# The routing table of the second expert layer: tokens alone, and gates by token

## The chip, the cores and the metric

The kernel runs on one core of one Trainium2 chip. The metric is the time of one execution on the device, in microseconds; lower is better. Runs before the change: 4362.11, 4370.67 and 4372.54 us, median 4370.67.

A core has five engines that run their own instruction streams in order and meet through semaphores: TensorE (PE; PEld is its weight load), VectorE (DVE), ScalarE (ACT), GpSimd (POOL) and SyncE (SP, which here only issues DMA transfers). Transfers issued by SP and ACT go through hardware queues, those issued by POOL (all indirect ones, gathers and scatters by a column of row numbers) through a software queue; all of them share 16 DMA engines.

## The reference, cut to what matters

A macaron block on x of shape 8 x 1024 x 512, that is T = 8192 tokens of 512 values: half an expert layer, attention, half an expert layer again with the same weights.

```python
x = x + 0.5 * _L0_ffn_ref(_layernorm(x), w_router, w_gate, w_up, w_down)
x = x + _L0_attn_ref(_layernorm(x), ...)          # 16 heads of 32
x = x + 0.5 * _L0_ffn_ref(_layernorm(x), w_router, w_gate, w_up, w_down)
```

The expert layer sends each token to the one expert (of 32) with the largest logit. Each expert takes at most C = 320 tokens, in the order of the tokens; those that come later get nothing added.

```python
probs = softmax(xt @ w_router)
top1 = argmax(probs);  gate = probs[top1]
pos = cumsum(onehot(top1))[token, top1] - 1       # place among the expert's tokens
accepted = pos < C
slot = where(accepted, top1 * C + pos, E * C)
buf[slot] = xt
y = (silu(buf @ w_gate) * (buf @ w_up)) @ w_down  # per expert
out = xt + where(accepted, y[slot] * gate, 0)
```

So two things belong to a place (expert, position): the number of the token that has it, and that token's gate. The change is about how these two come to the second layer's experts.

## The kernel before, in words

**First layer.** `front` normalizes and routes all 64 tiles of 128 tokens. It ends with `rows_of`: the token numbers by place, turned by a product on PE (`pt`) into a column of 128 row numbers for each block of 128 places, sorted by how full the experts are. They are kept as `come` (which rows to gather) and `go` (where to scatter). The gates, one per token, go to a DRAM tensor `gates`. Then `experts` branches (`tc.Switch`) on a register that every engine loads from `arm`: it picks one of four lists of widths, for experts that are more or less full. In the branch `Expert.keep` takes over `come` and `go`, and `feed` calls `fetch_gates` for each expert: two or three indirect gathers on POOL, of 128 gates each, by the token numbers in `come` (82 in all).

**Attention.** `Attention.run` goes through stages of 16 slots. In each slot the order of the engines is written out by hand (`manual_schedule`; SP alone is left to the compiler's planner): scores, exponents and weighted sums for one group of four heads, the row maxima of the next, and smaller tasks that are cut up with `yield` and take turns by rank. A task yields `WAIT, n` for n slots, `DVE, n` for a share of DVE's time in a slot, `PE, n` for a place on PE. One such task is `finished(b, half)`, which calls `Block.route` for four tiles of tokens as soon as their logits are there. There are 16 of them; the last two (b = 7, half 0 and 1) come in the last stage and in `ending`.

`route` computes the largest logit, the one-hot matrix, the place of each token (a scan over tiles, two products on PE), from it `slot` (the row of the table), then waits in `scaled` for the rows' mean and variance, and takes the exponent on ACT and from it the gate. Then `put` scatters, with four indirect transfers on POOL, pairs of (token, gate), held in `entries`, to the rows of a DRAM table. The last group (`late`) does it in two steps: the pair with a zero for the gate is scattered once `slot` is known, while the rows are still being finished; the gates go later, in `Late.put`, into a second table `late.table`, from inside the branch.

**Between attention and the second layer.** The last group's `route` also gives the ranks of the experts (`sorted`: `matrix`, `order`, `arm`). `ending` issues the load of the first expert's `w_gate` (1 MB) once `order` is there, and adds the last four tiles' rows to x2. Then comes the branch of `experts`. Inside it `Expert.places` reads the table (96 rows of 128 pairs, L778), copies the half-filled last blocks (L779), turns the token numbers by a product (L788), writes `come` (L790), and yields; the first expert's rows are gathered with `come` (L875), normalized and transposed in `begin`, and its products start (L969). After the gather of the second expert's rows, `late.put` scatters the last gates (L745) and the second table is read (`more`, L783). At the end of the first expert's gated products, `then` calls the last part of `places`: it adds `more`, turns the gates by a second product, and writes `go`. `quarters` does the same again, in small, for the experts whose last block is scattered in quarters.

The start of the kernel fills both tables: `none` and `nothing` are set by POOL and written to DRAM by ACT's queue (L2129, L2132).

## Time and profile before

| | us |
|---|---|
| median of the timed runs | 4370.67 |
| the profiled execution | 4346.86 |
| its span | 4345.1 |
| front of the first layer | 0 to 119 |
| experts of the first layer, to the last scatter | to 877 |
| attention's slots | about 912 to 3549 |
| join: last routing, table, gather, first products | 3549 to 3589 |
| experts of the second layer | to 4345 |

In the profile, times count from the span's start. A line such as `3572.12 0.35 SPq L778 DMA_DIRECT2D slots<-table x1` reads: start, duration (for a DMA, its issue on the queue, not the transfer), engine or queue, line of the kernel, operation, output from input, count; what stands in brackets behind is how long the engine was idle before, and what ended that. In the chain of waits, each piece is released by the one before it. In a table of stretches, each engine has its busy time and, in brackets, its number of instructions; then follow the clock granted to PE as a share, the share of the DMA engines that is busy, and GB/s.

### The profile page before, as it was taken

How to read it: one execution, taken by the hardware profiler on the slowest of the kernel's cores; microseconds unless marked ns; L12 is line 12 of the kernel's file. 1: busy time of each engine (PE TensorE's matmuls, PEld its weight loads, DVE VectorE, ACT ScalarE, POOL GpSimd, SP SyncE). 2: the span in 40 equal slices, each digit the busy share in tenths (PEclk: the TensorE clock that was granted, in tenths of full speed). 3: DMA queues.
4: the chain of work that ended last, by engine and by line, in shares of the span. 5: the costliest groups of instructions: out<-in, count | busy, mean ns of one | idle time of the engine just before them, and what ended most of it. 6: DMA issues, size and time to landing. Idle time of an engine off the chain costs nothing.

```text
span 4345.1 us, 84352 instructions
## 1 busy us (share of the span) xinstructions
PE 4233.0 (97%) x32310; PEld 2407.5 (55%) x32310; DVE 2600.6 (60%) x4964; ACT 2616.9 (60%) x4325; POOL 1401.0 (32%) x1640
## 2 busy tenths in 40 slices
PE   8899999979999999999999999999999979999999
PEld 6566777844444444444444444444444436667777
DVE  8434433356766776876876776776866754344333
ACT  6112221237888888888888888888888842112121
POOL 7344444421222242242232232232232213333332
PEclk9999999989999999999999999999999989999999
DMA  4656666531112212212212212212212116566664
GB/s 157 217 185 204 206 204 229 197 111 48 50 42 71 79 46 65 80 48 65 77 48 65 79 47 65 81 47 63 80 42 60 38 59 206 191 202 202 217 228 162
DMA packets 310835, 495.59 MB, mean 114 GB/s; under 512 B 65049, under 2 KB 99235, under 8 KB 310418
## 3 DMA queue, kind: packets, MB, share of 16 engines
q1 hardware_dynamic: 269698, 412.06, 31.0%
q0 software_dynamic: 39776, 76.77, 5.5%
q8 instruction: 257, 4.21, 0.4%
q14 instruction: 160, 1.31, 0.1%
q10 hardware_dynamic: 944, 1.23, 0.1%
HBM read 379.85 MB, written 87.93 MB: 108 GB/s over the span
## 4 chain that ended last, share of the span: by engine, by line
PE 91%; DVE 3%; issue 2%; ACT 1%; POOL 1%; DMA 1%; POOLq 0%; ACTq 0%; SPq 0%; DVEq 0%
PE s L1240 11%; PE s L1842 11%; PE s L1221 11%; PE gp L969 10%; PE up L969 10%; PE s L1910 10%; PE s L1813 10%; PE yp L1015 9%; PE s L1806 4%; PE tp L957 2%; PE yp L1023 1%; DVE nm L1850 1%; ACT s L1854 1%; PE s L207 1%; DVE st L164 1%
## 5 line engine op out<-in xcount | busy, mean ns | idle before, releaser
L1850 DVE TENSOR_REDUCE nm<-s 128x1 f32<-128x1024 f32 x1024 | 1205.6, 1219 | 541.7 <-PE s L1842 540.3
L1854 ACT ACTIVATE s<-s,nm 128x1024 f32<-128x1024 f32 x1024 | 1114.3, 1088 | 149.9 <-DVE nm L1850 141.3
L974 ACT ACTIVATE sg<-gp 128x320 f32<-128x320 f32 (+7 forms) x256 | 99.5, 389 | 1061.8 <-PE gp L969 1060.8
L1820 ACT ACTIVATE pr<-s 128x512 f32<-128x512 f32 x992 | 538.1, 594 | 230.7 <-PE s L1813 226.8
L1748 POOL TENSOR_TENSOR raw<-raw,a 128x512 f32<-128x512 f32 x125 | 158.6, 1269 | 1312.6 <-DMA rot<-raw 957.3
L1842 PE MATMUL s<-cross,swapped 32*128 32x512 f32 x2048 | 560.4, 607 | 5.4 <-DMA cross<-k 3.1
L1842 PE MATMUL s<-k,q 32*128 32x512 f32 x2048 | 560.1, 603 | 0.0
L1822 ACT ACTIVATE pr<-s 128x1024 f32<-128x1024 f32 x528 | 542.9, 1031 | 19.7 <-PE s L1813 19.7
L1813 PE MATMUL s<-q,k 32*128 32x512 f32 x4096 | 538.4, 590 | 0.0
L1221 PE MATMUL s<-hT,wqk 128*32 128x128 f32 (+3 forms) x4720 | 503.3, 324 | 8.8 <-ACT pr L1820 4.9
L1910 PE MATMUL s<-pr,big 128*32 128x512 f32 x4096 | 492.7, 598 | 0.5 <-ACT pr L1822 0.5
L969 PE MATMUL gp<-bT,wg 128*128 128x272 f32 (+7 forms) x1984 | 488.7, 389 | 0.0
L969 PE MATMUL up<-bT,wu 128*128 128x272 f32 (+7 forms) x1984 | 484.9, 387 | 0.0
L1221 PEld LDWEIGHTS s<-hT,wqk 128*32 128x32 f32 (+1 forms) x4720 | 299.1, 129 | 286.1 <-ACT pr L1820 101.6
L1015 PE MATMUL yp<-wd,a 128*128 128x512 f32 x992 | 445.9, 592 | 0.0
L969 PEld LDWEIGHTS gp<-bT,wg 128*128 128x128 f32 x1984 | 371.6, 190 | 87.4 <-issue 21.4
L969 PEld LDWEIGHTS up<-bT,wu 128*128 128x128 f32 x1984 | 374.4, 190 | 70.3
L996 DVE TENSOR_TENSOR a<-sg,up 128x320 f32<-128x320 f32 (+7 forms) x256 | 110.6, 432 | 491.0 <-PE up L969 431.5
L1842 PEld LDWEIGHTS s<-k,q 32*128 32x128 f32 x2048 | 243.2, 183 | 102.0 <-DVE raw L1689 36.3
L1910 PEld LDWEIGHTS s<-pr,big 128*32 128x32 f32 x4096 | 106.7, 109 | 347.6 <-ACT pr L1820 187.4
L1019 DVE SCALAR_TENSOR_TENSOR ys<-yp,gates,x 128x512 f32<-128x512 f32 x128 | 96.1, 751 | 336.9 <-PE yp L1015 336.9
L1842 PEld LDWEIGHTS s<-cross,swapped 32*128 32x128 f32 x2048 | 224.4, 183 | 119.3 <-DVE raw L1689 22.8
(307 smaller groups left out, 5394.8 us busy)
## 6 DMA issues: line engine op xcount, KB each, us to landing
wg<-in_w_gate SPq DMA_DIRECT2D x62, 1024.0 KB
wu<-in_w_up SPq DMA_DIRECT2D x62, 1024.0 KB
wd<-in_w_down SPq DMA_DIRECT2D x62, 1024.0 KB
rot<-raw SPq DMA_DIRECT2D x1000, 32.0 KB
all<-in_x SPq DMA_DIRECT2D x32, 512.0 KB
xt<-first_rows SPq DMA_DIRECT2D x64, 256.0 KB
swapped<-q SPq DMA_DIRECT2D x256, 64.0 KB
xr<-first_rows SPq DMA_DIRECT2D x64, 256.0 KB
```

The costliest lines, as they stand in the source:

```text
L969: nc.tensor.matmul(acc, w[:, k, f * P : (f + 1) * P], to.bT[:, k, 0:width], start=(k == 0), stop=(k == s.KD - 1),)
L1015: nc.tensor.matmul(yp, a[:, f, i * P : (i + 1) * P], wd[:, f, :], start=(f == 0), stop=(f == KF - 1),)
L1221: self.nc.tensor.matmul(acc[a : a + w, lo:hi], one[:, a : a + w], two[:, lo:hi], start=(i == 0), stop=(i == len(terms) - 1),)
L1240: self.nc.tensor.matmul(bank[a : a + w, 0 : to - at], one[:, a : a + w], two[:, at:to], start=(i == 0), stop=(i == len(terms) - 1),)
L1806: nc.tensor.matmul(sb[:, h, :], self.ones16[at : at + 3, :], row[at : at + 3, :], start=True, stop=False,)
L1813: nc.tensor.matmul(sb[:, h, :], k[at, t * P : (t + 1) * P], q[at, n * 512 : (n + 1) * 512], start=False, stop=True,)
L1820: nc.scalar.activation(pr[:, h, :], sb[:, h, :], AF.Exp)
L1822: nc.scalar.activation(pr, sb, AF.Exp)
L1842: nc.tensor.matmul(sa[:, m, :], (own if here else swapped)[at, at_q], ka[at, m * 512 : (m + 1) * 512] if here else cross[at, :], start=Tru ...
L1850: nc.vector.tensor_reduce(nm[:, j, h : h + 1], flat, AX.X, ALU.max, negate=True)
L1854: nc.scalar.activation(flat, flat, AF.Exp, bias=nm[:, j, h : h + 1], accum_out=se[pair][:, j, odd : odd + 1],)
L1910: nc.tensor.matmul(po[at : at + HD, :], self.v[b][t + j][:, c * P + at : c * P + at + HD], prs[h // 2 * 2][:, h % 2, :], start=(j == 0), s ...
```

## The change

The second layer is given its places and gates in the form that the first layer has.

- The table holds the token alone (one number in place of two); it is filled with `none` alone, and the second table, `Late`, `entries` and `places` are gone.
- `route` has new arguments. For all groups but the last, `put` comes right after `scaled` and ahead of exponent and gate; for the last, it comes once `slot` is known, as before. The gates of every group are kept in `gate` and stored to a DRAM tensor by token, `gates[1]`: by SP, one slot after the gate's instructions, and by ACT for the last group. Each store writes 128 x 4 single numbers.
- A new function, `Attention.placed`, is called after `finish` and ahead of the branch: it reads the table, copies the half blocks, turns the tokens by one product and writes `come` and `go` into tiles that last through the branch.
- In the branch, `Expert.keep` serves both layers; `fetch_gates` now also runs for each of the second layer's experts (82 more gathers of 128 gates on POOL), and nothing is turned any more after the first expert's gated products. `quarters` turns one matrix, not two.

The diff, cut to its core:

```diff
@@ Block.constants
-        self.entries = pool.tile([P, self.NT, 2], F32, name="entries")
+        self.gate = pool.tile([P, self.NT], F32, name="gate")
...
-        nc.vector.tensor_copy(self.entries[:, :, 0], self.token)
@@ Block.route
-        row = self.entries[:, t0 : t0 + G, :]
+        gate = self.gate[:, t0 : t0 + G]
...
                 nc.gpsimd.indirect_dma_start(
                     out=table[t0 + j],
                     out_offset=bass.IndirectOffsetOnAxis(ap=slot[:, j : j + 1], axis=0),
-                    in_=row[:, j, :],
+                    in_=self.token[:, t0 + j : t0 + j + 1],
                     in_offset=None,
                 )
...
-        if late:
-            nc.vector.memset(row[:, :, 1], 0.0)
-            yield from put()
+        r = None if last else (yield from scaled())
+        yield from put()
         if ordered:
             at_once(ordered())
-        r = yield from scaled()
+        if last:
+            r = yield from scaled()
         yield DVE, 0.3
         nc.vector.tensor_tensor(ex, ex, over_e(r), ALU.mult)
         nc.scalar.activation(ex, ex, AF.Exp)
         yield WAIT, 1
         yield DVE, 0.7
-        gate()
-        if not late:
-            yield from put()
+        nc.vector.tensor_reduce(se, ex, AX.X, ALU.add)
+        nc.vector.reciprocal(se, se)
+        nc.vector.tensor_scalar(gate, se, 0.5, None, ALU.mult)
+        if not last:
+            yield WAIT, 1
+        (nc.scalar if last else nc.sync).dma_start(store, gate)
@@ Block.experts
-                if kept:
-                    expert.keep(kept)
-                else:
-                    places = expert.places(table, late)
-                    next(places)
+                expert.keep(kept)
                 now = expert.gather(0, widths[0])
...
-                if late:
-                    late.put(nc)
-                    next(places)
-                    then = lambda: next(places, None)
@@ Expert.feed
-        if self.of is not None:
-            self.fetch_gates(now)
+        self.fetch_gates(now)
...
-        if then:
-            then()
@@ Attention.run
                 self.ending()
                 self.finish()
+                self.placed()
                 self.apart()
...
+    def placed(self):
+        nc, s, pool, E, n = self.nc, self.s, self.ranking, self.s.E, self.s.last
+        R = s.NB * E
+        rows = pool.tile([R, P], F32, name="rows")
+        come, go = (pool.tile([P, R], I32, name=name) for name in ("come", "go"))
+        self.kept = SimpleNamespace(rows=rows, come=come, go=go, gates=self.gates)
+        nc.sync.dma_start(
+            rows, self.whole_table[0 : s.NS, :].rearrange("(r s) c -> r (s c)", s=P)
+        )
+        nc.vector.tensor_copy(rows[R - E : R, n:P], rows[R - E : R, 0:n])
+        pt = self.take()[:, 0:R]
+        nc.tensor.matmul(pt, rows, self.ranks[0], start=True, stop=True)
+        nc.vector.tensor_scalar(come, pt, float(s.T - 1), None, ALU.min)
+        nc.vector.tensor_copy(go[:, 0 : R - E], pt[:, 0 : R - E])
+        for i in range(2):
+            p = slice(i * n, (i + 1) * n)
+            nc.vector.tensor_scalar(
+                go[p, R - E : R], pt[p, R - E : R], 2.0, float(i), ALU.mult, ALU.add
+            )
@@ Attention.finished
-            late=self.late if last and half else None, spaced=not last,
+            self.gates[first * P : (first + 4) * P, :].rearrange("(t p) c -> p (t c)", p=P),
+            spaced=not last, last=last and half,
@@ tile_macaron
-    table = dram.tile([s.NS + T, 2], F32, name="table")
-    gates = dram.tile([T, 1], F32, name="gates")
+    table = dram.tile([s.NS + T, 1], F32, name="table")
+    gates = [dram.tile([T, 1], F32, name=f"gates{i}") for i in range(2)]
...
-        nothing = pool.tile([P, s.NS // P], F32, tag="nothing", bufs=1, name="nothing")
-        nc.gpsimd.memset(nothing, 0.0)
-        nc.scalar.dma_start(
-            late.table[0 : s.NS, :].rearrange("(p r) c -> p (r c)", p=P), nothing
-        )
```

## The prediction

> **What bounds the kernel now.** I read the page first (part 4, the chain that ended last), then the busy time by stage, then the timeline and the waits around the two joins. The profiled execution took 4346.86 us (span 4345.1 us and 1.76 us around it); the median of the timed runs is 4370.67 us, 23.8 us above. The sum is made against the profiled time, and that offset is added unchanged.
>
> The chain by engine, from the page: TensorE carries nearly all of it.
>
> ```profile
> PE 91%; DVE 3%; issue 2%; ACT 1%; POOL 1%; DMA 1%; POOLq 0%; ACTq 0%; SPq 0%; DVEq 0%
> ```
>
> By stretch (columns: length, busy PE, PEld, DVE, ACT, POOL with counts, clock, DMA share, GB/s): first layer, attention, the join behind it, second layer.
>
> ```profile
> 131.00:895.00 764.00, 749.71 (x3359) 533.60 (x3358) 290.55 (x775) 157.59 (x280) 330.43 (x351) 0.99 0.62 205
> 950.00:3549.00 2599.00, 2578.44 (x24716) 1238.65 (x24718) 1870.49 (x2966) 2210.96 (x3562) 707.35 (x839) 1.00 0.22 59
> 3549.00:3589.00 40.00, 13.71 (x49) 7.80 (x42) 22.20 (x90) 3.80 (x7) 16.04 (x19) 0.63 0.49 155
> 3589.00:4346.00 757.00, 745.78 (x3346) 530.72 (x3345) 282.93 (x752) 152.67 (x273) 250.10 (x260) 0.99 0.61 200
> ```
>
> In attention PE is busy 99.2%, so nothing that leaves PE fed changes it. In the 40 us of the join PE works 13.7 us: only there, at the very start and in the first expert can this change pay.
>
> The join in the timeline: first and last scatter of the last four tiles, the weight load, the table's read, its copy, the places, the first gather, the first product.
>
> ```profile
> 3561.27 0.96 POOL L307 DMA_INDIRECT table<-entries,late_slot  x1 [0.30 <-DVE both L639]
> 3561.64 0.42 SPq L671 DMA_DIRECT2D big<-in_w_gate  x1
> 3565.06 0.95 POOL L307 DMA_INDIRECT table<-entries,late_slot  x1 [0.30 <-issue]
> 3572.12 0.35 SPq L778 DMA_DIRECT2D slots<-table  x1
> 3574.45 0.22 DVE L779 COPY slots<-slots 32x128 f32<-32x128 f32 x1 [3.90 <-DMA slots<-table]
> 3575.96 0.26 DVE L790 TENSOR_SCALAR come<-pt 128x96 int32<-128x96 f32 x1 [1.29 <-PE pt L788]
> 3577.11 1.03 POOL L875 DMA_INDIRECT x<-x,come  x1 [8.23 <-DMA all<-x]
> 3588.51 3.33 PE L969 MATMUL gp<-bT,big 128*128 128x320 f32 x8
> ```
>
> The queue SP itself stood for the landing of these scatters (total, times, longest):
>
> ```profile
> SPq L778 <- DMA table<-entries,late_slot: 5.6, 2, 5.1
> ```
>
> So the path is: slots of the last tiles (written 3558.10 to 3558.26) -> POOL free (3561.27) -> scatters landed (some 3570.8) -> read -> turn -> gather -> product. The branch is not on it: SP was at the read by 3565.7 (3570.8 less the 5.1 us wait).
>
> **The change, part by part.**
>
> *The start.* The chain runs through ACT's issue of the second table's zeros:
>
> ```profile
> 6.41 1.14 ACTq L2132
> 7.58 1.28 ACT L546
> ```
>
> ACT then works without a gap to 27.5, and DVE waits for it twice (2.25 us at 19.36, about 1.4 at 27.72) before it becomes the engine that paces the front. The issue goes, and with it the fill `nothing` (0.17 us on POOL) and a 0.20 us copy on DVE; ACT can load its table at about 6.2. Bounds: 0 (the first products, at 8.25, are late next) to -1.4. I take -1.0, since DVE's two waits can absorb more than that.
>
> *The 15 groups routed before the last.* Their scatters (4 x 1.0 us on POOL each) go ahead of exponent and gate; POOL's waits for the gate, 84.4 us over 15 groups, disappear. POOL has 707 us of work in 2599, so this is worth 0. Added are 15 stores on SP, each 512 single elements of 4 B. SP's issue: a weight load of as many runs takes 0.37 to 0.42 us. On the DMA engines: the window 3556 to 3561.6 has nothing but 8 B scatters,
>
> ```profile
> q0 software_dynamic: 109, 0.00, 1.6%
> ```
>
> 1.6% of 16 x 5.6 us over 109 packets is 13 ns each, so 512 packets are 0.42 us of each engine. Behind a store on SP stand the copies for the rotation, `swapped` and `cross`, whose reader is PE. In 2637 us of attention PE waited for `cross` once, 3.1 us; so they arrive with time to spare, and 0.8 us per store is hidden: 0. If that cover fails: 15 x 0.8 = 12 us. A store may also stand on SP for its gate; POOL stood 5.6 us per group for it: that is the slower rival below.
>
> The Trainium skill (DMA: Bandwidth & Descriptors, Rules for kernel authors) speaks against such a store: a strided last dimension becomes one descriptor per element, and it advises making it contiguous. The same page (Anatomy of one DMA) puts 2.0 us of fixed cost on a DMA; 15 of them in sequence on the path would be an estimated 30 us and a slower kernel. The row above, and that nobody waits for a store until 3592, make it nothing.
>
> *Scatters of the last two groups.* Those of the group before the last no longer wait for the gate (3555.65): POOL is free after the power at 3550.64, their slots are there since 3549.2. So they run from 3550.9 to 3555.9 instead of 3556.11 to 3560.96, and the last four start at about 3558.4 and 3562.2, not 3561.27 and 3565.06: 2.8 us earlier. Their landing is what counts. Scatters issued up to 3560.01 landed in 2.1 us; the four from 3561.27 on took 5.6 to 7.6, median 6.6, beside 2 MB of `w_gate` and rows of x2 (282 to 400 GB/s from 3564 to 3570). The last one now starts 0.6 us behind the load's issue, nearest to the row at 3562.54, so I give it 6.6 us: landed 3568.9, read issued 3569.4 with half a us of semaphores. Bounds: landed in 2.1 us, the read at 3565; or in 7.6 with today's 1.3 us of semaphores, at 3571. Gain 2.7, between 1 and 7.
>
> *Read and turn ahead of the branch.* The read (48 KB, was 96) meets the end of that traffic: 2.33 us today in a quiet moment, up to 4.8 (a gather under load); I take 2.6, a loss of 0.3. Copy, product and `come` keep their 1.8 us. POOL passed its branch by 3571.4 and needs `come` at about 3573.8, so its first gather follows 0.9 us later as today. What is moved past: SP's branch now follows the read and took 3.6 us (3562.06 to 3565.7), so the two loads `all` (0.5 MB each) go out at about 3573.4 beside the gathers rather than ahead of them. The first layer has this order, and there gather to product took 11.9 us (119.11 to 130.99) against 11.4 here: a loss of 0.5 to 1.0, I take 0.7. DVE's branch follows its writing of `go`; it is at most 3.9 us (3570.54 to 3574.45), against some 4.3 us until the first gathered rows land, so it is just covered; at worst +1.5. PE's has 8 us. ACT gets the last store (at 3570.6, 0.5 us) ahead of its branch and is needed at 3580. Join: -2.7 + 0.3 + 0.7 = -1.7, bounds -5 and +1.5.
>
> *The experts.* The first layer fetches its gates by token already, so it is the measurement of the new form. There the first expert runs from the last half of its products straight into the transposes and the down product:
>
> ```profile
> 147.15 2.15 PE up L969 x8
> 149.30 0.66 PE tp L957 x6
> 149.96 3.43 PE yp L1015 x8
> ```
>
> The second layer has the turn of the gates in between:
>
> ```profile
> 3604.76 2.17 PE up L969 x8
> ...
> 3607.51 0.21 DVE slots L785
> ...
> 3607.99 0.48 PE pt L788 x2
> ```
>
> From the first `gp` to the last scatter the first layer takes 746.27 us (131.04 to 877.31), the second 748.37 (3588.57 to 4336.94). The 2.10 us are this turn and the second product of the quarters, and both go. The 82 gate fetches (0.98 us and 0.27 of issue on POOL, 103 us) lie beside PE: POOL's 330 of 764 us in the first layer shows that they fit. If POOL were full, they would cost up to 103. -2.1, between -2.4 and -1.5. On POOL the four late scatters (3591.24 to 3596.1) also leave the way of the next expert's weight load; it was in time before: 0.
>
> Sum: -1.0 + 0 - 1.7 - 2.1 = -4.8 us: 4342.1 for the profiled execution, 4365.9 for the median.
>
> **The rivals.**
> 1. *The join gives nothing.* The scatters land when the weight load lets them, whenever issued, and the branches of DVE and SP become visible behind the turn. For it: a 5.1 us wait for landing, beside 1 MB of weights; against it: 2.1 us for those issued a us before the load. -1.0 - 2.1 + 0 to 1.5: 4367.6 to 4369.1.
> 2. *Everything early lands early.* Last scatter in 2.1 us, the join takes -5, the start -1.4, and the earlier POOL saves a few of PE's 20 us of waits in attention: 4358 to 4362.
> 3. *Slower: SP is held up in attention.* A store is queued ahead of the rotation's copies and stands for its gate. The price is the 5.6 us that POOL stood per group, 84 us in all; it decides once more than 18 of them reach PE (1.2 per group), since -4.8 must be undone and 13 passed. A third of it gives 4394. Against it: PE's one wait of 3.1 us for `cross`; for it: nothing in this trace bounds how SP's order comes out.
> 4. *The fetches fill POOL* in the second layer: up to +103; the first layer speaks plainly against it.
>
> **How the numbers follow.** Chances: the forecast 0.53, rival 1 0.23, rival 2 0.11, rivals 3 and 4 0.13. What a measurement here tells from no change is about 0.3%, 13 us. The forecast and rival 1 lie within it but for the spread of runs (4362.1 to 4372.5); of rival 2 most of it too. Faster 0.11, same 0.75, slower 0.14. The forecast's own range, -5 to +1.5 at the join with the other bounds and 4 us of spread, is 4357 to 4373. The range reaches up toward rival 3 to leave out no more than 2 in 10, and below through rival 2: 4354 to 4382.
>
> **What would show it.** Right: ACT's first table load near 6.2; scatters of the last group from 3558, the read near 3569, the first gather near 3575 and the first `gp` near 3586 (each less about 1 for the start); the first `up` of the second layer followed by `tp` at once; 746 us from first `gp` to last scatter. Wrong: the read still at 3572 (landing set by the weights), DVE's first statistics late after landed rows (branch exposed), PE waits on `cross` or `swapped` in attention with SP standing for `gate`, POOL without gaps in the second layer.

## The result, and the profile after

The changed kernel took 4414.73 us (median of 4 runs, 4410.22 to 4415.05), the kernel before beside it 4368.27 us (4 runs): ratio 1.0104, 95% interval 1.009 to 1.0118. It is 46 us slower. The forecast was 4365.9 us in a range of 4354 to 4382, with a chance of 0.14 for slower.

One thing is needed to read the numbers below. The runs were made on six occasions, each with its own runs of the kernel before, and these fall into two kinds: the kernel before took 4367 to 4368 us on four of them (the result's among them) and 4354 us on two (single runs there reach down to 4345). I call them H and L. All ratios are between runs of one occasion; the few differences in us that cross from the result's occasion to the next are between two with the same 4368 us for the kernel before. The profile that the prediction used, 4346.86 us, is like an L profile; the timed runs beside it were like H. A later profile of the kernel before in kind H (4370.82 us) is the one to put beside the profile after (4415.05 us, span 4413.3).

The chain of the profile after reads nearly as before; TensorE still carries it.

```profile
PE 90%; DVE 4%; issue 3%; ACT 2%; DMA 1%; POOL 1%; SPq 0%; POOLq 0%; DVEq 0%; ACTq 0%
```

By stretch (length, busy PE, PEld, DVE, ACT, POOL with counts, clock, DMA share, GB/s), the changed kernel: first layer, attention, join, second layer.

```profile
131.00:895.00 764.00, 750.19 (x3360) 534.02 (x3359) 291.33 (x776) 157.92 (x280) 330.74 (x351) 0.99 0.62 205
950.00:3608.00 2658.00, 2619.32 (x24700) 1253.92 (x24699) 1878.00 (x2959) 2211.68 (x3564) 707.07 (x839) 0.99 0.22 58
3608.00:3661.00 53.00, 18.12 (x75) 8.78 (x74) 26.21 (x103) 5.80 (x10) 16.45 (x19) 0.60 0.46 112
3661.00:4413.00 752.00, 745.36 (x3342) 530.64 (x3340) 283.58 (x744) 152.74 (x272) 326.68 (x338) 1.00 0.61 202
```

The same for the kernel before in kind H, without the first layer:

```profile
950.00:3568.00 2618.00, 2595.56 (x24701) 1245.44 (x24703) 1873.51 (x2958) 2211.02 (x3564) 708.09 (x839) 0.99 0.21 59
3568.00:3612.00 44.00, 18.00 (x73) 9.43 (x69) 24.67 (x100) 5.27 (x8) 15.60 (x19) 0.64 0.46 144
3612.00:4368.00 756.00, 746.75 (x3347) 531.42 (x3346) 283.57 (x753) 153.25 (x274) 250.86 (x260) 0.99 0.60 200
```

PE has as many products in attention (24700 and 24701) and takes some 40 us more for them. To cut the stages alike in each kernel I take as marks the start of the last scatter into `first_rows`, the start of PE's last product that reads `mrow`, the first product of the second layer and the start of its last scatter, and call what follows to the end of the span the tail:

| profile | us | to the first mark | attention | join | second layer | tail |
|---|---|---|---|---|---|---|
| before, as predicted from | 4346.86 | 877.3 | 2668.0 | 43.2 | 748.4 | 8.2 |
| before, kind H | 4370.82 | 877.6 | 2690.3 | 44.1 | 748.9 | 8.1 |
| after, kind H | 4415.05 | 878.2 | 2730.4 | 51.8 | 747.0 | 5.9 |
| difference, both H | 44.2 | +0.6 | +40.1 | +7.7 | -1.9 | -2.2 |

So the loss is in attention, where the sum had 0, and in the join, where it had -1.7. What was forecast for the experts came. One caution for the column on attention: in every profile its first stretch (from the mark to the last `rot<-s,a` on DVE) takes either 40.1 to 40.5 or 43.3 to 43.8 us, long before the first of the scatters and stores in question. That alone is worth 3 to 4 us between two profiles. The two in kind H here both have the long form, the one that the prediction used has the short one.

Inside attention the loss shows in one group of products of PE (engine, operation, tiles, shape, count; busy us and mean ns; idle time before them and what ended it), between 1000 and 3500 us. After:

```profile
L1758 PE MATMUL s<-mrow,ones 3*128 3x512 bf16 x1936 | 211.0, 385 | 25.1 <-ACT s L1806 14.4 <-issue 10.7
```

Before, kind H:

```profile
L1806 PE MATMUL s<-mrow,ones 3*128 3x512 bf16 x1976 | 211.4, 385 | 11.9 <-ACT s L1854 11.6 <-issue 0.2
```

New are 10.7 us in which PE stood for "issue", nothing that the profile shows. They lie in six of the eight batches (the kernel takes its tokens in eight batches of 1024), each time inside a row of six scatters that POOL runs one behind the other (1887.23 to 1893.59 in the second batch, 1.26 us apart). Before, POOL waited for each group's gate between them; now it comes from the wait for the rotation's rows, finds six scatters ready and runs them at once. The planned spacing of one slot between two scatters orders the instructions, it does not space them in time.

The join after, in the timeline: the store of the last group but one, the weight load, the last scatter, the last store, the read of the table, its copy, the first gather, the first product.

```profile
3619.42 0.37 SPq L343 DMA_DIRECT2D gates<-gate  x1
...
3624.79 0.41 SPq L668 DMA_DIRECT2D big<-in_w_gate  x1
...
3625.65 0.95 POOL L301 DMA_INDIRECT table<-token,slot  x1 [0.30 <-issue]
...
3634.08 0.38 ACTq L343 DMA_DIRECT2D gates<-gate  x1
3637.64 0.33 SPq L1290 DMA_DIRECT2D rows<-table  x1
...
3646.81 0.19 DVE L1293 COPY rows<-rows 32x64 f32<-32x64 f32 x1 [12.76 <-DMA rows<-table]
...
3649.07 1.03 POOL L807 DMA_INDIRECT x<-x,come  x1 [16.69 <-DMA all<-x]
...
3660.44 1.97 PE L901 MATMUL gp<-bT,big 128*128 128x320 f32 x3
```

```profile
3625.00:3628.00 3.00, 2.50 (x3) 0.41 (x2) 2.86 (x7) 0.00 (x0) 1.30 (x2) 0.50 0.62 38
3628.00:3631.00 3.00, 0.00 (x0) 0.00 (x0) 2.86 (x7) 0.00 (x0) 0.00 (x0) 0.50 0.38 18
3631.00:3634.00 3.00, 0.00 (x0) 0.00 (x0) 1.36 (x9) 0.31 (x1) 1.04 (x1) 0.50 0.78 81
3634.00:3637.00 3.00, 0.00 (x0) 0.00 (x0) 0.05 (x1) 0.00 (x0) 0.00 (x0) 0.50 1.06 402
```

The second fence is the stretches from 3625 to 3637, columns as above. The scatters went out at 3621.88 to 3625.65, 13.2 us behind the end of attention instead of 16.0 in the profile that the prediction used: 2.8 us earlier, as forecast (3.6 us against the profile in kind H). But behind the store the weight load moves 38, 18 and 81 GB/s instead of the 282 to 400 that it had before, and reaches 402 only at 3634. SP stood for the landing of the scatters 12.2 us in all (5.6 before):

```profile
SPq L1290 <- DMA table<-token,slot: 12.2, 3, 6.8
```

The read then goes out 3.6 us behind the store of the last group on ACT's queue and takes from 3637.64 to 3646.81, 9.2 us, where it took 2.33 before. Two stores are at work here; the run with one of them alone, further down, shows what belongs to the first.

### The profile page after: what moved, and what is told of

Read it like the earlier page. It is cut to its first block, busy times and chain, and to the rows that moved or that the text cites. A ratio compares the mean times of both kernels' runs of the same rounds, so it can differ in the third digit from the quotient of the medians.

```text
span 4413.3 us, 84426 instructions
## 1 busy us (share of the span) xinstructions
PE 4278.9 (97%) x32306; PEld 2424.4 (55%) x32306; DVE 2610.0 (59%) x4956; ACT 2617.6 (59%) x4325; POOL 1477.4 (33%) x1716
## 4 chain that ended last, share of the span: by engine, by line
PE 90%; DVE 4%; issue 3%; ACT 2%; DMA 1%; POOL 1%; SPq 0%; POOLq 0%; DVEq 0%; ACTq 0%
PE s L1170 11%; PE s L1794 11%; PE gp L901 10%; PE s L1151 10%; PE up L901 10%; PE s L1862 10%; PE s L1765 10%; PE yp L944 9%; PE s L1758 4%; PE tp L889 2%; PE yp L952 1%; DVE nm L1802 1%; ACT s L1806 1%; DMA table<-token,slot 1%; PE s L206 1%
## 5 line engine op out<-in xcount | busy, mean ns | idle before, releaser
L1794 PE MATMUL s<-cross,swapped 32*128 32x512 f32 x2048 | 576.9, 614 | 4.9 <-issue 3.1
L1794 PE MATMUL s<-k,q 32*128 32x512 f32 x2048 | 572.5, 610 | 1.1 <-DVE raw L1641 1.1
L1765 PE MATMUL s<-q,k 32*128 32x512 f32 x4096 | 555.5, 596 | 2.9 <-issue 2.7
L1151 PE MATMUL s<-hT,wqk 128*32 128x128 f32 (+3 forms) x4720 | 513.3, 327 | 4.6 <-DVE hT L1571 3.8
```

Of the source, the lines that this page charges most:

```text
L1151: self.nc.tensor.matmul(acc[a : a + w, lo:hi], one[:, a : a + w], two[:, lo:hi], start=(i == 0), stop=(i == len(terms) - 1),)
L1765: nc.tensor.matmul(sb[:, h, :], k[at, t * P : (t + 1) * P], q[at, n * 512 : (n + 1) * 512], start=False, stop=True,)
L1794: nc.tensor.matmul(sa[:, m, :], (own if here else swapped)[at, at_q], ka[at, m * 512 : (m + 1) * 512] if here else cross[at, :], start=Tru ...
```

## The experiments

Two suspects were in the trace after, the rows of scatters and the single-element stores, and each can be taken away alone. The first theories, as they are on record: A, rows of back-to-back scatters hold up PE; B, 512 single-element stores block the DMA engines.

### Taking each away (occasion of kind H, before 4368.19 us)

**The scatters behind the gate again.** The scatter's source `pos` is written behind the gate, so that POOL waits for it as before; the stores stay.

```diff
-                    in_=self.token[:, t0 + j : t0 + j + 1],
+                    in_=self.token[:, t0 + j : t0 + j + 1] if last else pos[:, j : j + 1],
...
-        yield from put()
+        if last:
+            yield from put()
...
+            nc.vector.scalar_tensor_tensor(
+                pos, gate, 0.0, self.token[:, t0 : t0 + G], ALU.mult, ALU.add
+            )
+            yield from put()
```

> The changed kernel, with the scatters of all groups but the last made to wait for the gate again, as in the kernel before (they take the token from a tile that is written after the gate); the stores of single gates stay. Theory A (bursts: six scatters back to back on POOL hold up PE's next refill of instructions, PE starves and its clock drops): no refill later than about 15 us, attention from 2663 back to about 2600 us, the join still 8 us longer than before; about 4355 us where the changed kernel takes 4414. Theory B (stores: 512 single elements written to 2 KB of DRAM block the DMA engines, the refill among them): attention stays near 2660, about 4414.

Measured: 4376.33 us, ratio 1.0018 (1.0008 to 1.0027). Attention 2696.4 us instead of 2730.4, join still 52.2. The profiled execution (4382.19) is the slowest of ten. The waits for the gate that the prediction valued at 0 were worth some 38 us against the result's 4414.73.

**The gates turned on PE and stored once.** The 16 stores go; one transpose in `placed` and one store of 64 rows of 512 B take their place. The scatters stay early.

```diff
-        if not last:
-            yield WAIT, 1
-        (nc.scalar if last else nc.sync).dma_start(store, gate)
...
+        gt = self.take()[0 : s.NT, 0:P]
+        nc.tensor.transpose(gt, s.gate, s.ident)
+        turned = pool.tile([s.NT, P], F32, name="turned")
+        nc.scalar.copy(turned, gt)
+        nc.scalar.dma_start(self.gates.rearrange("(t p) c -> t (p c)", p=P), turned)
```

> The changed kernel, with the sixteen stores of single gates taken out; the gates of all groups are turned once on PE after the table's places and stored in 64 runs of 512 B. Scatters run early as in the changed kernel. Theory A: attention still about 2660 us with clock dips, only the join gains: weight load and table read no longer stand, read to landing 2 to 3 us and not 9, so some 8 to 10 us less than the changed kernel, about 4405. Theory B: the dips go too, about 4345 to 4355.

Measured: 4389.81 us, ratio 1.005 (1.0033 to 1.0066). The join is 38.9 us, 5.2 less than before in kind H: without the stores the earlier scatters do bring what the prediction hoped for. Attention is 2714.2 us, still 24 more than before in kind H (27 behind its first stretch, which is short here).

**Both edits.**

> The changed kernel with both edits: scatters after the gate, and gates turned and stored in runs of 512 B. Both theories: attention about 2600 us and a join no longer than before; by the terms of the prediction that held (first expert and quarters -2, join -2 to 0) 2 to 4 us under the kernel before. If attention stays long here, neither theory is right.

Measured: 4357.88 us, ratio 0.9979 (0.9968 to 0.9989): faster than both kernels. Attention 2683.8, join 42.1. Against this kernel the early scatters cost 31.9 us (4389.81 less 4357.88) and the stores 18.5 us (4376.33 less 4357.88). The changed kernel, which has both, is 46 + 10 = 56 us above it, so the two together cost about 6 us more than their sum (this last number goes across two occasions).

**The kernel before with its scatters early.** The gate is left out of the scattered pairs but for the last 512 tokens, so that the scatter need not wait for it. No stores.

```diff
-            nc.vector.tensor_scalar(late.gate if late else row[:, :, 1], se, 0.5, None, ALU.mult)
+            nc.vector.tensor_scalar(late.gate if late else se, se, 0.5, None, ALU.mult)
...
-        if late:
-            nc.vector.memset(row[:, :, 1], 0.0)
-            yield from put()
+        r = None if late else (yield from scaled())
+        yield from put()
```

> The kernel before with one part of the change alone: the scatters of pairs (8 B) of all groups go ahead of exponent and gate. No stores of single gates. It leaves out the gates of all tokens but the last 512 (their place in the table is zero). Theory A: six scatters back to back, attention 50 to 65 us longer than before, about 4420. Theory B, and also a theory that only 4 B entries do it: attention as before, about 4365.

Measured: 4398.91 us, ratio 1.0064 (1.0046 to 1.0081), attention 2722.3 us. The early scatters alone, put into the old kernel, make most of the loss: 30.7 us here with 8 B each, 31.9 with 4 B in the comparison above, so size and table make no difference that can be seen.

### What in the row? (occasion of kind L, before 4353.68 us)

**The last batch's first half early as well**, the candidate for the best version. In the other batches the scatters stay behind the gate.

```diff
-        if last:
+        if not spaced:
             yield from put()
...
-        if not last:
+        if spaced:
             nc.vector.scalar_tensor_tensor(
```

> The kernel with both edits (4357.88), and in the last batch alone the first half's four scatters go ahead of the gate again, as in the change. In it nothing follows that PE could starve on for long: the bursts of the other seven batches stay spaced by their gates. Theory A (back-to-back scatters cost only where PE needs refills under load; the join gains from earlier scatters): attention as with both edits, 2684 +-5; the join 39 us (38.9 with the gates turned) instead of 42.1; time 4354 to 4356. Rival (a burst costs some 4 us wherever it stands, also in the last batch): 4358 to 4360.

Measured: 4344.12 us, ratio 0.9982 (0.9973 to 0.9991); join 39.9 us, as expected. The time itself is not what was expected, because the occasion was another.

**No planned spacing behind the gate** (both edits kept): rows of four, late.

```diff
-                if j and spaced:
-                    yield WAIT, 1
```

> The kernel with both edits (4357.88), but the four scatters of a half are issued one after the other behind the gate, with no slot of the planner between them. They are as late as before, but bursts of four, 14 of them. Theory A (it is the row of scatters without a gap that delays PE's refill, whenever it comes): 7 bursts of six cost some 30 us with the gates turned, 4.3 each; by the number of scatters 14 bursts of four cost up to 2.9 each: 4375 to 4400, with refill gaps of 16 us and more beside the bursts and PE stalled by issue. Rival (going ahead of the gate is what costs, a different order on DVE, ACT or SP): as with both edits, 4355 to 4363.

Measured: 4346.29 us, ratio 0.9987 (0.9978 to 0.9996). Rows of four, no pause of PE in any.

**POOL held without DMA** (both edits kept): four powers of 128x4 where the change has its early scatters.

```diff
+        else:
+            held = narrow("held")
+            for j in range(G):
+                if j and spaced:
+                    yield WAIT, 1
+                nc.gpsimd.tensor_tensor(held, s, self.power[:, 0:G], ALU.pow)
```

> The kernel with both edits (4357.88), and where the change put its early scatters, four powers of 128x4 on POOL instead (1.04 us each by the row of rstd, the length of a scatter, but no DMA); the scatters stay behind their gates. POOL gets 60 more instructions and 62 us. Theory A1 (the scatters' DMA elements stand ahead of PE's refill): as with both edits, 4355 to 4365, no refill gap over those seen there. Theory A2 (POOL is held for some 7 us without a gap, and something that PE needs waits for POOL): attention +30 as with the gates turned, 4383 to 4393.

Measured: 4345.67 us, ratio 0.9988 (0.9979 to 0.9997), attention 2671.7. No loss. (Only four powers stood in a row, 4 us, since a scatter with its gate came between them and the rest.)

**The kernel before once more.**

> The kernel before once more, unchanged, for its profile: the profile that the prediction used was 4346.86 us, below every timed run (4360 to 4372). If the stalls of PE at the refill that the change shows come by chance in the kernel before as well, an execution of about 4365 us has two to four of them in attention, with attention of 2680 to 2690 us in place of 2668, and the other stages the same within 1 us. If the offset lies elsewhere (the start or the layers), attention stays at 2668.

Measured: 4355.13 us, attention 2675.2; no pause in it. The three results look as if theory A and its rival A2 were settled. The next occasion showed that they were not.

### The control (occasion of kind L, before 4353.61 us)

**The early scatters diluted**, a power on POOL behind each (on top of the kernel with the gates turned):

```diff
                     in_offset=None,
                 )
+                if spaced:
+                    nc.gpsimd.tensor_tensor(held, s, self.power[:, 0:G], ALU.pow)
```

> The kernel with the gates turned (scatters early, no single stores: 1.005 of before, attention 2714), and behind each early scatter a power of 128x4 on POOL (1.04 us, no DMA). The row of six then has a scatter every 2.3 us instead of every 1.26; POOL is held longer, 14 us instead of 7.5, and has 15.8 us until the rotation needs it next. Theory A (it is how closely the scatters' DMAs follow each other that stalls PE): the pauses of some 0.4 to 1.1 us between PE's instructions inside the row go, the time is that of the kernel with both edits, 0.997 to 0.999 of before. Rival E (what costs is that the scatters come ahead of the gate, with another order on POOL, DVE and ACT): 1.004 to 1.006 of before, as with the gates turned.

Measured: 4344.89 us, ratio 0.9983 (0.9973 to 0.9993).

**A row of eight, late, as planned** (both edits kept): in POOL's order the first half's scatters are put behind the second half's gate.

```diff
+            if not spaced:
+                put()
+            elif t0 % 8 == 0:
+                self.first_half = put
+            else:
+                self.first_half()
+                put()
```

> The kernel with both edits, but the first half's four scatters of a batch wait for the second half's gate, and all eight go out in a row: late, and closer together than in any kernel so far. Theory A: the pauses of PE come back in every batch but the last, 7 rows of eight against 6 rows of six: 1.004 to 1.010 of before. Rival E (early is what costs): 0.997 to 0.999 of before. The kernel with rows of four late lost nothing (0.9987), so a third way is that the length of the row does not matter in this place, which also gives 0.997 to 0.999; only together with the kernel diluted above are the two told apart.

Measured: 4345.00 us, ratio 0.9987 (0.9977 to 0.9996). But the edit did not make rows of eight. The order on POOL changed; the first half's scatters still wait for their own gate alone, and the second half's for theirs. In seven batches the trace has two rows of four, 8 to 13 us apart, as in the second batch, where the fourth and the fifth scatter are:

```profile
1879.49 0.96 POOL L299 DMA_INDIRECT table<-pos,slot  x1 [0.31 <-issue]
1884.26 0.96 POOL L299 DMA_INDIRECT table<-pos,slot  x1 [3.81 <-DVE pos L341]
```

So this run is a second one on rows of four, and no row longer than six was tried in attention.

**The gates turned, the same kernel as above.**

> The kernel with the gates turned once more, unchanged, beside the others on the same chip: 1.005 of before, with PE's pauses inside six rows of scatters (18 us of PE's gaps in attention against 6 in the kernel before). If the stalls belong to a chip and not to the kernel, 0.997 to 0.999.

Measured: 4346.28 us, ratio 0.9986 (0.9976 to 0.9995), where the same kernel had 1.0050. Its six rows of six are there (14.2 to 20.6 us behind the first scatter of the second batch, 14.6 to 21.0 the first time), and PE does not pause in them. So on an occasion of kind L no row shows a cost, and the runs on rows of four, on POOL held and on dilution, all made there, tell nothing about what in the row matters. The control belonged on the same occasion from the start.

The pair is the best view of the cost, though: one kernel, the same place of the program. Set side by side by the order of DVE's instructions, the two executions keep step up to the first row of six (-0.03 us), part by 6.1 to 8.8 us at each of the six rows, and then keep step again (43.6 and 43.8 us): the whole difference in attention lies at the rows. Kind H, the second batch (start, us, engine, line, operation):

```profile
1881.78 0.96 POOL L301 DMA_INDIRECT table<-token,slot  x1 [0.30 <-issue]
1881.82 1.06 PE L1148 MATMUL s<-hT,wqk 128*32 128x128 f32 x32
...
1883.04 0.96 POOL L301 DMA_INDIRECT table<-token,slot  x1 [0.30 <-issue]
...
1883.48 0.37 PE L1760 MATMUL s<-mrow,ones 3*128 3x512 bf16 x1 [0.60 <-issue]
...
1884.20 0.37 PE L1760 MATMUL s<-mrow,ones 3*128 3x512 bf16 x1 [0.36 <-issue]
1884.30 0.95 POOL L301 DMA_INDIRECT table<-token,slot  x1 [0.30 <-issue]
...
1885.63 0.37 PE L1760 MATMUL s<-mrow,ones 3*128 3x512 bf16 x1 [1.05 <-issue]
...
1886.35 0.58 PE L1760 MATMUL s<-mrow,ones 3*128 3x512 bf16 x1 [0.35 <-issue]
...
1886.36 2.66 PE L1767 MATMUL s<-q,k 32*128 32x512 f32 x5
...
1888.05 0.35 DVE L1643 TENSOR_SCALAR raw<-s,bias 128x128 f32<-128x128 f32 x1 [5.18 <-remote]
```

and the stretches around it:

```profile
1882.00:1884.00 2.00, 1.25 (x34) 0.79 (x26) 0.87 (x2) 1.62 (x4) 1.70 (x2) 1.00 0.39 69
1884.00:1886.00 2.00, 0.74 (x2) 0.09 (x1) 0.00 (x0) 0.00 (x0) 1.39 (x2) 1.00 0.51 63
1886.00:1888.00 2.00, 1.65 (x7) 1.02 (x9) 0.00 (x0) 0.00 (x0) 0.52 (x1) 0.60 0.01 0
...
1890.00:1892.00 2.00, 2.00 (x8) 0.50 (x2) 0.36 (x1) 1.17 (x2) 0.00 (x0) 0.50 0.03 8
```

Kind L:

```profile
1874.82 0.95 POOL L301 DMA_INDIRECT table<-token,slot  x1 [0.30 <-issue]
1874.93 1.06 PE L1148 MATMUL s<-hT,wqk 128*32 128x128 f32 x32
...
1875.92 0.40 PE L1760 MATMUL s<-mrow,ones 3*128 3x512 bf16 x4
...
1876.08 0.96 POOL L301 DMA_INDIRECT table<-token,slot  x1 [0.30 <-issue]
1876.15 1.03 PE L1767 MATMUL s<-q,k 32*128 32x512 f32 x8
1876.16 0.34 DVE L1643 TENSOR_SCALAR raw<-s,bias 128x128 f32<-128x128 f32 x1
```

```profile
1876.00:1878.00 2.00, 2.00 (x21) 0.82 (x21) 1.04 (x5) 1.68 (x4) 1.62 (x2) 1.00 0.80 115
```

In kind L the four products of `mrow` run within 0.40 us, and at 1876.16 DVE reads what PE left. In kind H they start at 1883.48, 1884.20, 1885.63 and 1886.35; with their weight loads (1882.81, 1883.50, 1884.91, 1886.33) that is about one instruction per 0.7 us, with no wait on record. DVE, which needs only the 32 products from 1881.82, goes on at 1888.05, 5 us late. PE's signal for these products is on record at 1887.96, 5.1 us behind their (modelled) end; in kind L it comes 0.05 us behind. So it was not the issue alone that was held up, but also work that PE, by its records, had already begun. The stretches show what follows: PE busy 1.25, 0.74 and 1.65 of 2 us, and then the clock at 0.50, with a PE that is busy throughout and works at half speed. Setting the two kernels' products side by side by their place in the program, the lag that this row adds is 3.8 us at the last of the four `mrow` products and 7.6 us once the clock is back: half of the cost is the pauses, half the clock. That answers the period of a batch, 330.8 us in kind H and 323.3 in kind L, 7.5 us.

The clock's record has it at 0.50 from 1886.4 to 1893.2, 6.8 us (the stretches above have 0.60 from 1886 to 1888, 0.50 after that), behind 3.5 us of broken work (1882.88 to 1886.35) in which PE ran three products of 0.37 us. The Trainium skill (TensorE: Matmul & The Clock Gate, the section on the HAM clock gate) has PE at half its clock after an idle window of some 3.4 us. The length agrees; but here PE was not idle, only little used.

The pair also corrects theory A where it named PE's refill of instructions (packets of 16 KB on the queue that the profile calls instruction, one per 12.9 us). In kind H the refills around this row start at 1872.40 and 1890.03. PE issues without the pauses again from 1886.35, with no refill in between. So a refill did not end the pauses; that the next one is late fits PE's slow progress.

**One store at the join put back** into the candidate, on SP, into a tensor that nobody reads.

```diff
         nc.vector.tensor_scalar(gate, se, 0.5, None, ALU.mult)
+        if not spaced and not last:
+            yield WAIT, 1
+            nc.sync.dma_start(store, gate)
```

> The kernel with both edits and the last batch's first half early (0.9982 of before, join 39.9 us), with one of the change's 16 single-element stores put back: that of the last batch's first half, on SP ahead of the expert's weight load, into a tensor that nobody reads. The prediction had such a store at 0.42 us of the engines. Theory B (512 single elements of 4 B slow the loads and scatters behind them for some ten us): the weight load creeps for 8 us or more, the scatters land late, the join takes 47 to 52 us, the time rises by 7 to 12 us: 1.000 to 1.001 of before. Rival (the store was harmless; the last store, on ACT, or the scatters themselves made the join long): join 40 to 41 us, 0.998 of before.

Measured: 4346.55 us, ratio 0.9988 (0.9979 to 0.9998); join 43.5 us against 39.9 without the store. SP's total wait for the scatters, with the store and without:

```profile
SPq L1296 <- DMA table<-token,slot: 11.2, 3, 5.3
```

```profile
SPq L1293 <- DMA table<-token,slot: 7.4, 3, 4.7
```

3.6 us for one store, also in kind L: neither the 7 to 12 of theory B nor nothing. The slow load is there with this one store, at 35 GB/s in the second stretch behind its issue; without the store it has 268:

```profile
3565.00:3568.00 3.00, 0.00 (x0) 0.00 (x0) 2.83 (x7) 0.00 (x0) 0.00 (x0) 0.50 0.92 35
```

```profile
3570.00:3573.00 3.00, 0.00 (x0) 0.00 (x0) 2.86 (x7) 0.00 (x0) 0.00 (x0) 0.96 0.78 268
```

The join alone shows the cost (one profile each; without single stores and with the last scatters early it is 38.6 to 39.9 in the five profiles with the new table). The two times, 2.4 us apart and from two occasions, do not.

### The change again (two occasions of kind H, before 4367.45 and 4367.00 us)

> The changed kernel once more, unchanged. Theory D (the pauses of PE inside the rows of scatters come on some chips and not on others; the single-element stores cost something on each): on a chip like that of the last two calls the attention is 5 to 20 us longer than before (the stores alone), the join 47 to 52 us, the layer 1.5 us shorter, in all 1.001 to 1.005 of before, and no pause of 0.7 us and more per instruction on PE inside a row; on a chip like the first 1.009 to 1.011, as measured. Rival (the stores and the early scatters together make the pauses, and the kernel with the gates turned was only near the edge): 1.008 to 1.011 on either chip, with pauses.

Measured: 4404.60 us, ratio 1.0076 (1.0057 to 1.0095), a little under both ranges; attention 2723.6, join 50.9, pauses in all six rows.

> The changed kernel with its scatters behind the gates, once more: only the stores are left of what was held to cost. Measured first 1.0018, against 0.9979 with both edits: 0.39% for 16 stores. If a store costs the same on each chip, 1.001 to 1.003 here, with a join of 50 to 53 us and refills of 3 us and more behind the stores. If it costs only on the first chip, or only the one at the join (3.6 us for one there), 0.998 to 1.000.

Measured: 4376.80 us, ratio 1.0020 (1.0010 to 1.0029), as the first time; attention 2687.5, join 49.6.

> The kernel before, for its profile on the chip of this call. On a chip like that of the last two calls 4345 to 4357 us with no pause of PE inside a batch. On a chip like the first 4360 to 4372 us; the 15 to 25 us over the profile that the prediction used are then to be seen as pauses of PE or as times of lower granted clock in attention (theory D), or in the layers (then the two chips differ in something else).

Measured: 4370.82 us. This is the profile shown above. Its additional time sits where the scatters are, though all of them are behind their gates here. Kind H, POOL's second and fifth scatter of the second batch:

```profile
1879.08 1.01 POOL L307 DMA_INDIRECT table<-entries,slot  x1 [0.16 <-issue]
...
1890.63 0.96 POOL L307 DMA_INDIRECT table<-entries,slot  x1 [6.97 <-DVE entries L301]
```

Kind L:

```profile
1878.01 1.00 POOL L307 DMA_INDIRECT table<-entries,slot  x1 [0.15 <-issue]
...
1888.10 0.96 POOL L307 DMA_INDIRECT table<-entries,slot  x1 [5.52 <-DVE entries L301]
```

From the one to the other it is 11.55 us in kind H and 10.09 in kind L, and the period of a batch 324.9 and 323.1 us. Set side by side by their place in the program, PE's lag builds up between 13.9 and 15.7 us behind the first scatter (in kind L's times), from the third of three close scatters on (10.1, 12.4 and 13.7). So in kind H the kernel before pays 1.5 us for its row of three where the kernel with the gates turned pays 7.5 for its row of six. The same comparison over all of attention: 1.3 to 2.2 us at each of the six rows of three, 4.7 at the one row of four (from 3496.6, with the clock at 0.50 from 3502.2), and nothing to speak of at pairs and single scatters; together that is the 15.1 us between 2690.3 and 2675.2. The candidate, run again below, shows the same against its run in kind L: 1.3 to 2.3 us at its rows of three and 4.7 in the last batch.

> The kernel before with its scatters of 8 B ahead of the gate, the gates left out of all but the last 512 tokens, once more. It was 1.0064 on the first chip, with PE's pauses in six rows. Theory D: on a chip like that of the last two calls the pauses are gone and the time is that of before, 0.998 to 1.001; on one like the first 1.005 to 1.008. Rival (the size of 8 B or the second table makes them): 1.005 to 1.008 on either.

Measured: 4397.41 us, ratio 1.0061 (1.0042 to 1.0080), with the pauses, as the first time.

> The changed kernel a third time, unchanged. The occasions so far are of two kinds: on two of them the kernel before took some 4368 us, on two 4354. Theory D (the kind of occasion decides whether a row of scatters on POOL makes PE pause): if before takes some 4368 us here, 1.007 to 1.011 with pauses, as before; if it takes 4354 us, no pauses of 0.4 us and more in the rows, and what is left is the stores: 1.001 to 1.004. Rival (the stores together with the early scatters make the pauses on any occasion): 1.007 to 1.011 also where before takes 4354 us.

Measured: 4404.41 us, ratio 1.0083 (1.0065 to 1.0101): the occasion was of kind H once more. What the change costs in kind L was therefore not measured.

> The kernel with both edits and the last batch's first half early, which was 0.9982 of before where before took 4354 us. It has no row of more than three scatters in attention and no single-element store. Theory D: where before takes 4368 us as well it is below before: 0.996 to 0.998 (with both edits alone 0.9979 there, less 3 us at the join); where before takes 4354 us 0.9975 to 0.9990 again. Rival (its early scatters of the last batch make PE pause on the first kind of occasion): 0.9985 to 1.001 there.

Measured: 4359.37 us, ratio 0.9984 (0.9974 to 0.9994); attention 2683.7, join 39.5. The candidate is 0.16 to 0.18% below the kernel before on both kinds. In kind H it can't be told from the kernel with both edits alone (0.9979).

### What is shown and what stays open

Shown: in kind H the kernels with early scatters (the change, the gates turned, the kernel before with early scatters) cost 28 to 38 us over the same kernel with the scatters behind the gate, in five comparisons (4414.73 against 4376.33, 4389.81 against 4357.88, 4404.60 against 4376.80, 4398.91 against 4368.19, 4397.41 against 4367.45; the first goes across two occasions), and PE pauses inside their rows. The granted clock says the same: between 1500 and 3300 us it falls to 0.50 six times, once per row of six, in each of the six profiles of these kernels in kind H, not once in the profile of the gates turned in kind L, and none to two times in the five profiles in kind H with the scatters behind the gate. Shown as well: the stores cost 16 to 25 us there (1.0020 against 0.9984 of 4367, 4376.33 against 4357.88, and 4414.73 against 4389.81); they are made up of 7 to 13 us at the join (49.6 against 42.1 and 51.8 against 38.9) and, behind attention's first stretch, of 0.4 (2558.3 against 2557.9 us from PE's first to its last product of `mrow`) to 13 us (2600.5 against 2587.6). What stores cost in attention is not traced to a wait.

Open: what distinguishes the two kinds. It is not the chip alone, for the control and the repeats ran on a chip of one number, and the DMA packets of each size take the same mean time on either. One sign goes with the kind without exception. The kept traces in kind H hold 55309 to 56097 records of semaphore updates (eleven profiles), those in kind L 60467 to 61797 (nine), with the same number of instructions (the gates turned: 55694 against 61757, 84400 instructions in each). The profile that the prediction used has 60487. In attention records go missing at the rows (2335 against 2706 from 1800 to 1950 us, and 2373 against 2388 in the 150 us ahead); in the expert layers more go missing, and these take the same time. Whether the recording has a part in the pauses, or only suffers from the same cause, no run separates. Open too is what counts in a row. Being early is not needed for a cost, for the rows of three and four behind the gate cost in kind H as well. For length and closeness speak that the pauses begin at the third scatter, and some 1.5 us for three, 4.7 for four, 7.5 for six. But place counts too: with the gates turned, in kind H, the row of four at 3513.2 costs 0.1 us. No run in kind H varied one of these alone. And what holds PE to an instruction per 0.7 us is not on record.

## Why the prediction was wrong, point by point

- **The step that failed: "The 15 groups routed before the last", cost 0.** Its first half called POOL's 84.4 us of waits for the gate worth 0 because POOL has time to spare. The wait did nothing for POOL, but it kept scatters apart, and nobody asked what six of them do when they come together. That POOL would run them in a row could be read from the profile of before: it stood 5.23 us for the rotation's rows with the scatters planned behind that. The price could not: that profile is like kind L, where a row costs nothing. With it fell the sentence that nothing that leaves PE fed changes attention: at the pauses no input of PE came late on record, and PE still stood and then ran at half its clock. Measured: 28 to 38 us in kind H and none that can be told in kind L (0.9986 with rows, 0.9982 without, on two occasions).
- **The same step's second half: "0.8 us per store is hidden: 0", at worst 12 us.** The row that priced a packet was right: 528 packets went by within 2 us, at 12.1% of 16 engines. What was mis-sized is what comes behind them: at the join a load that creeps, scatters and a read that land late. All in all the stores cost 16 to 25 us, 7 to 13 of it at the join for two of them and 0 to 13 in attention, so that the worst case was passed too. The prediction weighed a rule of the Trainium skill against its row (DMA: Bandwidth & Descriptors, Rules for kernel authors: make the last dimension contiguous) and put the rule aside. The measurement speaks for the rule: the same 32 KB as one store of 64 rows of 512 B, instead of 16 stores of single elements of 4 B, took 18.5 us off. (The edit changes number and place of the stores with their form; for the form alone no run was made.) The page's 2.0 us per DMA, which the prediction named beside it, is its fit for transfers issued from GpSimd; these 15 were issued by SP, and no run here measures a fixed cost for them.
- **The join: -1.7, bounds -5 and +1.5.** The order of events was right and the scatters went out 2.8 us earlier. Without the stores the join is 38.9 us against 44.1 in kind H and 38.6 against 43.2 in kind L, a gain of 5.2 and 4.6, at the favourable bound (which was added up a us short: 7 less 0.3 and 0.7 is 6, not 5). The read was issued 24.2 us behind the end of attention instead of 27.1 in kind L, so the -2.7 for the landing was right; it was the +0.3 and +0.7 for the read and the gathers beside `all` that were wrong. From the read to the first product it is 14.3 us instead of 16.1: the read takes 1.7 us instead of 2.4, and from the first gather to the first product it is 10.4 instead of 11.2. (In the other kernels without single stores the whole is 14.5 to 15.7.) With the stores the join is 51.8: the store, which the step let pass as free, is ahead of the load and the scatters on the engines.
- **The start: -1.0.** ACT's first table load did move, from 7.58 to 6.23:

```profile
6.23 1.28 ACT L543 ACT_TABLE_LOAD   x1 [6.23 <-POOL lane L359]
```

  but the first product of the experts stands at 131.5 us, not earlier than before (131.0; 130.4 to 131.6 over all profiles with the old table, 129.8 to 132.8 with the new). The bound of 0 was the answer.
- **The experts: -2.1, bounds -2.4 and -1.5.** Right in kind and nearly in size. From the first product to the last scatter it is 747.0 us against 748.9, and over all profiles 745.7 to 747.7 with the new form and 748.4 to 749.3 with the old, on average 1.9 us less. The turn of the gates between `up` and the transposes is gone, as the first layer had shown:

```profile
3677.10 2.32 PE L901 MATMUL up<-bT,big 128*128 128x320 f32 x8
...
3679.25 0.82 PE L889 MATMUL tp<-ident,b 128*128 128x128 f32 x6
...
3679.91 2.31 PE L944 MATMUL yp<-big,a 128*128 128x512 f32 x5
```

  POOL was busy 326.68 of 752 us with the fetches, so rival 4 fell as well.
- **The tail: not in the sum.** From the last scatter to the end the span has 5.9 us instead of 8.2, in each kernel with the new table, and 8.2 again where the kernel before got early scatters alone. The 2.3 us are a gain that no step named, and its cause was not tried.
- **The offset of 23.8 us "added unchanged".** It fits the two kinds of occasion: the profile is like one of L, in its time and in the records it holds, and the runs are like those of H. A profile of kind H beside it would have shown 1.3 to 2.3 us lost per batch at a row of three scatters, which was the warning. (The sum of the range has a slip as well: its upper bounds come to 0, which with 4 us of spread is 4374.7 and not 4373. Nothing hangs on it.)
- **Rival 3, slower through SP.** The sign was right and the mechanism was not: SP did stand for a gate, 47.6 us in ten waits, 9.6 of them for the last group but one, but no wait of PE for `cross` or `swapped` came of it in attention; PE stood for issue.
- **Rivals 1 and 2** fell with the stores. Without them the join has rival 2's number (-5), but not by its mechanism: the last scatter did not land in 2.1 us, for the read is issued 7.6 us behind it (3564.16 to 3571.75 in kind L; 7.1 before).

## What to carry to other kernels

A wait on an engine with time to spare may be what spaces its DMAs. Before taking it away, list what becomes ready together and will be issued in a row, and give such a row a price of its own, with a range that admits a loss, instead of the sum of its instructions. A store of single elements cost little here in the rows of its own packets and much in the transfers behind it; turn the data first where that is cheap. And where a profile lies outside the spread of the timed runs, find out why before building a sum on it, and run the control on each occasion.

## What the runs showed of the hardware that was not expected

- Inside a row of six indirect DMAs on POOL, 1.26 us apart, PE started one instruction per 0.7 us and lost 3.8 us on some occasions; the clock fell to 0.50 for 6.8 us behind it. On others the same program ran through the row without loss. The kind changes the unchanged kernel as well, 4368 against 4354 us, and the profiles of the two kinds differ by some 9% in the records of semaphore updates that they hold.
- The spells of half clock in attention last 3.4, 6.8, 10.2 or 17.1 us, multiples of 3.4, in all twenty profiles.
- A store of 512 elements of 4 B passes the DMA engines in 2 us, and a load of 1 MB issued 5.4 us later moved 38, 18 and 81 GB/s in its first three stretches of 3 us; with one such store put back into another kernel it was 30, 35 and 182, without it 18, 268 and 393.
- Powers of 128x4 on POOL, 4 us in a row beside the same products, cost PE nothing (in kind L: 0.9988 of before, no pause on record).
